# Six warming products, the first top between pair 1's two projections, and batch 1's feature sums as two VectorE instructions

## The chip, the cores and the metric

One core of a Trainium2 chip runs the whole kernel. Its engines are TensorE (PE, with its weight loads listed apart as PEld), VectorE (DVE), ScalarE (ACT), GpSimd (POOL) and SyncE (SP, which issues most DMAs). Each engine runs its own instructions strictly in the order in which the program lists them, and waits for the others through semaphores. The metric is the time of one execution on the device in microseconds, as the median of several runs; less is better.

## The reference

The input x is eight batches of 512 features by 1024 tokens; a 0/1 mask says for each token whether it is kept. Every batch gets one layer of attention with eight heads of 64 features, in which queries, keys and values are the same projection, and the result is added to x:

```python
xt = jnp.transpose(x, (0, 2, 1))
q = xt @ Wq.T
qh = q.reshape(B, T, NH, dk).transpose(0, 2, 1, 3)
scores = scale * jnp.einsum('bhqd,bhkd->bhqk', qh, qh)
logits = (scores * cmask + (1.0 - cmask) * NEG) * rmask
attn = jax.nn.softmax(logits, axis=-1)
ctx = jnp.einsum('bhqk,bhkd->bhqd', attn, qh)
out = ctx.transpose(0, 2, 1, 3).reshape(B, T, D) @ Wo.T
x = x + jnp.transpose(out, (0, 2, 1))
```

A token that is masked out as a query has all logits 0, so it attends to all tokens alike: its context is the projection of the mean token. A masked key gets no weight from the kept queries.

## The kernel before

About half of the tokens are kept, so the kernel gathers the kept tokens of each batch (at most 544) beside one column with the mean token, and does the attention on these alone. The work goes pair by pair: a pair is two heads (128 features) of one batch, so there are 4 pairs in a batch and 32 in all; pair number p below counts them through (pairs 0 to 3 are batch 0).

Ahead of the loop `early` works out the ranks of the kept tokens, turns batch 0 into token rows in DRAM (`turn_first`), and turns Wq on PE (`turn_weights`). `warm(n, block)` is n transposes of a block into a PSUM bank that nobody reads: PE work that computes nothing. There are three calls of seven, six and sixteen, and a last one of twenty behind the weights (L1231). `late` begins the main part: `gather` fetches batch 0's kept rows by five indirect DMAs (tile `xin`, issued by POOL, which then makes the masks `part` and issues the loads of batch 1 and of Wo), `put_mean` multiplies and places the mean column, and `collect` turns each gathered block on PE into `xc`, copied out of PSUM by ACT and DVE in turns.

A pair needs, in this order:

- `project(pair, hf)`, twice: four products with Wq for one half of the columns (L593, tile `pq`), and an ACT copy into the ring `qT` (L603, for the second half also L605).
- `values(pair)`: five PE transposes of `qT` (L621), copied by ACT into `v` (L627, L628).
- `lengths_of(pair)`: an ACT square of `v` (L638), the DVE sums by head (L640, tile `len`) and their maximum (L647, tile `top`).
- `bias_of(pair)`: `turn_top` turns the top on PE (L650), DVE takes the maximum and makes the bias of the exponentials (L659 to L662). This must stand ahead of the pair's first exponential.
- `scores(pair, c)` for five key blocks in the order 4, 0, 1, 2, 3: score products on PE (L701 for the short last block, L679 for the others) and the exponentials on ACT (L704, L687, tile `e`), each of which frees the PSUM buffer of its scores. There are two buffers of two banks.
- the products of exponentials and values (L725 and L743, tile `av`), spread over the next pair's blocks, DVE's inverses of the sums (L819 to L836), whose rows go through DRAM (SP), and the output.

The loop runs over pairs p and, inside, over k = 0 to 4, the place in the block order. At each k it issues first the scores, then the tasks that `slots_of(p)` has listed for this k, then pieces of later batches by tables keyed (pair in batch, k): loads, `turn` (DVE transposes L474, tile `xt`, and their stores to DRAM), `search` (DVE counting, L527), `gather`. So the order on each engine is written out by hand. For the mean token of batch b, the 1024 tokens of each feature are summed: `add_features(b, i)` is one ACT pass over 128 features and 512 tokens with an accumulator (L493, tile `junka`), eight of them for a batch. They run four and four: for batch 1 at (p, k) = (0, 3) and (1, 3), for later batches beside other pairs. Batch 0's sums are made instead by DVE, two instructions over 128 x 4 x 512 elements (L427 in `mean_first`). `mean_of` adds the two halves.

For pair 0, `late` runs both projections, the values, the lengths, both projections of pair 1 and then the bias; `slots_of(0)` gives pair 0's slots `values` of pair 1 at k = 0, its lengths and the first half of pair 2's projection at k = 1, and so on.

Of the kernel before, what the change touches and what calls it, by code (L numbers as in the profile page):

```python
# [10 lines left out]
F32 = mybir.dt.float32  # L11
# [295 lines left out]
def attention_of_kept_tokens(ctx, tc, x, mask, wq, wo, out, ident, wqT, woT, verdict, flag):  # L307


    nc = tc.nc  # L310
# [118 lines left out]
    def warm(n, block):  # L429
        pt = bank("warm")  # L430
        for i in range(n):
            nc.tensor.transpose(pt[:, :P], block, ident)
# [55 lines left out]
    def add_features(b, i):  # L488
        r, d = divmod(i, ND)
        if i == 0:  # L490
            xbars[b] = sb.tile([P, ND, NN], F32, tag="xbar", name=f"xbar_{b}")
        junk = sb.tile([P, NB], F32, tag="junka", name=f"junka_{b}_{i}", bufs=1)
        nc.scalar.activation(junk, xs[b][r][:, d, :], AF.Copy, accum_out=xbars[b][:, d, r : r + 1])  # L493

    def mean_of(b):

# [504 lines left out]
    def slots_of(p):  # L1001

        b, pr = pairs[p]
        todo = [[] for _ in range(NC)]
        before = pairs[p - 1] if 0 < p < len(pairs) - 1 else None
        behind = pairs[p + 1] if p + 1 < len(pairs) else None
        ahead = pairs[p + 2] if p + 2 < len(pairs) else None

        def do(k, f, *args):
            todo[k].append(lambda: f(*args))  # L1010

        late = p == 2
        new = pr == 2 and b + 1 < B
        by_vector = nc.vector.tensor_copy

        def project_with_values():
            project(ahead, 0, lambda end: turn_values(behind, end))
            copy_values(behind)

        def mean_with_values():  # L1020
            pt = bank(f"mean_{b + 1}")
            turn_values(behind, pt[:, KH : KH + P])
            put_mean(b + 1, pt, lambda: copy_values(behind))

        def project_with_top(hf, tag="t"):
            project(ahead, hf, lambda to: turn_top(behind, to), tag)
            bias_of(behind)

        if before:
            do(0, go_on_attend, before)  # L1030
        due = []
        if pr == 1 and b + 1 == B:
            due = [0, 1]
        elif pr > 0 and 0 < b < B - 1:
            due = {1: (0, 1, LAST), 2: (2,), 3: (3,)}[pr]
        if not new:
            for i in due:
                do(3, output, b - 1, i)
        if p == 0:
            do(0, values, behind)  # L1040
            do(1, lengths_of, behind)
            do(1, project, ahead, 0)
            do(2, project, ahead, 1)
            do(3, bias_of, behind)
        elif late:
            do(1, values, behind)
            do(2, lengths_of, behind)
            do(2, end_attend, before)
            do(2, put_mean, b + 1)
            do(2, collect, b + 1, 0)  # L1050
            do(3, bias_of, behind)
            do(3, collect, b + 1, 1, by_vector, "a")
            do(3, collect, b + 1, 2, None, "a")
            do(4, collect, b + 1, 3)
            do(4, collect, b + 1, 4)
            for hf in range(2):
                do(4, project, ahead, hf, None, "a")
        elif new:
            do(1, mean_with_values)
            do(2, end_attend, before)  # L1060
            do(3, collect, b + 1, 0, by_vector)
            do(3, collect, b + 1, 1, by_vector)
            do(3, collect, b + 1, 2, by_vector, "a")
            do(3, collect, b + 1, 3, None, "a")
            do(3, collect, b + 1, 4, by_vector)
            do(3, lengths_of, behind)
            for i in due:
                do(3, output, b - 1, i)
            do(3, project_with_top, 0)
            do(3, project, ahead, 1, None, "a")  # L1070
        elif ahead:
            do(1, project_with_values)
            do(2, lengths_of, behind)
            do(2, end_attend, before)
            do(3, project_with_top, 1)
        elif behind:
            do(1, output, b - 1, LAST - 1)
            do(1, values, behind)
            do(2, lengths_of, behind)
            do(2, end_attend, before)  # L1080
            do(3, bias_of, behind)
            do(3, output, b - 1, LAST)
        if p == ND - 1:
            for d in range(ND):
                do(3 + d // 2, turn_weights, woT, "wo", d, None, "at"[d // 2], True)
        if pr == 1 and b + 1 == B:
            do(4, output, b - 1, 2)
        if p + 1 == len(pairs):
            for i in range(NC):
                do((1, 1, 2, 3, 4)[i], begin_output, b, i)  # L1090
        return todo
# [30 lines left out]
    def early(n):  # L1122
# [105 lines left out]
            order_columns(e, nc.vector.tensor_copy if e % 2 else nc.scalar.copy)  # L1228
        for d in range(ND):
            turn_weights(wqT, "wq", d, nc.vector.tensor_copy if d % 2 else nc.scalar.copy)  # L1230
        warm(20, weights["wq"][ND - 1][:, 0:P])  # L1231

    def place_all():

# [22 lines left out]
    def late(n):  # L1257
# [13 lines left out]
            project(pairs[0], hf)  # L1271
        values(pairs[0])
        lengths_of(pairs[0])
        for hf in range(2):
            project(pairs[1], hf)
        order = [LAST, *range(LAST)]
        bias_of(pairs[0])

# [23 lines left out]
        for p, pair in enumerate(pairs):  # L1302
# [3 lines left out]
            for k, c in enumerate(order):  # L1306
                scores(pair, c)
                if k == 1:
                    add_ends(pair)
                if k == 0 and p > 1:  # L1310
                    contexts(pairs[p - 2])
                if k == 0 and before:
                    if p + 1 < len(pairs):
                        invert(before)
                    else:
                        inv = inverses(before)
                if p + 1 == len(pairs):
                    if k == 1:
                        spread(before, inv)
                        contexts(before)  # L1320
                if b > 1:
                    for i in FETCH.get((pr, k), ()):
                        keep_step(pair, c)
                        fetch(b - 2, i)
                if b + 1 == B:
                    for i in FETCH_LAST.get((pr, k), ()):
                        keep_step(pair, c)
                        fetch(b - 1, i)
                for i in (GATHER if b else GATHER_LATER).get((pr, k), ()) if b + 1 < B else ():
                    keep_step(pair, c)  # L1330
                    gather(b + 1, i)
                if k == 3 and (p == 0 or pr in (1, 3)):
                    to = b + 2 if pr == 3 else b + 1
                    for i in range(G) if to < B else ():
                        add_features(to, (G if pr == 1 else 0) + i)
                for task in todo[k]:
                    task()
                if b + 1 < B:
                    at = TURN if b else TURN_LATER
                    if pr < 2 and (pr, k) in at:  # L1340
                        turn(b + 1, at.index((pr, k)))
                    if pr == 1 and k == 4:
                        mean_of(b + 1)
                    for i in () if b else LATER.get((pr, k), ()):
                        search(b + 1, i)
                    if pr == 2 and k == 2:
                        queries_of(b + 1)
                if b + 2 < B:
                    if pr == 3 and (pr, k) in TURN:
                        turn(b + 2, TURN.index((pr, k)))  # L1350
                    for i in LOAD.get((pr, k), ()):
                        load_piece(b + 2, i)
                    if pr == 1 and k == 4:
                        load_ranks(b + 2)
                    for i in SEARCH.get((pr, k), ()):
                        search(b + 2, i)
                if b > 0:
                    for i in (ROWS if b + 1 < B else ROWS_LAST).get((pr, k), ()):
                        load_rows(b - 1, i)
                if p == 0 and k == 1:  # L1360
                    place_all()
                if p == 1 and k == 4:
                    turn_places()
                if b > 1:
                    for i in FINISH.get((pr, k), ()):
                        finish_blocks(b - 2, i)
                if b + 1 == B:
                    for i in FINISH_LAST.get((pr, k), ()):
                        finish_blocks(b - 1, i)
                issue_stores()  # L1370
                while rests:
                    rests.popleft()()
                    if b + 1 < B:
                        break
# [129 lines left out]
```

## Time and profile before

| | |
|---|---|
| median of 3 runs | 659.57 us (658.69 to 660.84) |
| the profiled execution | 660.24 us; span from first to last instruction 658.5 us |
| busy over the span | PE 618.8 us (94%), PEld 383.9, DVE 355.7, ACT 383.6, POOL 212.0 |
| granted PE clock, mean | 0.98 |
| DMA | 116.61 MB, 177 GB/s over the span |
| last 20 warming products | start 25.6 to 27.7 us |
| four `junka` passes each | from 49.3 us and from 63.9 us |

The profile is one execution. A row of the timeline has the start and length in microseconds, the engine, the line of the kernel, the operation, the tile written and the tiles read, the shape, and the count of instructions merged into it. In brackets stand the idle time of the engine just ahead of the row and what released it, as far as the semaphore events tell; "issue" is a wait for nothing that the profile shows, "remote" one without a releaser among the core's instructions. Matrix products of float32 show as two rows each on PE, and their ends are modelled.

### The profile page before, as it was taken

To read this page: it belongs to the slowest core of one execution; us is meant where nothing else is said; L and a number is where in the kernel's file an instruction comes from. 1 tells how busy PE (TensorE), PEld (TensorE's weight loads), DVE (VectorE), ACT (ScalarE), POOL (GpSimd) and SP (SyncE) were. 2 spreads that over 40 slices of the span, in tenths; PEclk is the share of its full clock that TensorE was granted. 3 is DMA by queue.
4 is the path that set the end of the run, shared out by engine and by line. 5 is a ranking of instruction groups with operands and counts; after the bars stand their busy time and mean duration, and the time that the engine had idled before them with its cause. 6 is when DMAs were issued, how large, how long until landed. Compare 5 with 4: busy or idle time off the path is not lost. (4 is left out here: it accounts for less than half of the span.)

```text
span 658.5 us, 15960 instructions
## 1 busy us (share of the span) xinstructions
PE 618.8 (94%) x6092; PEld 383.9 (58%) x6092; DVE 355.7 (54%) x1032; ACT 383.6 (58%) x1020; POOL 212.0 (32%) x313
## 2 busy tenths in 40 slices
PE   5799799999999999999999999999999999998963
PEld 4765476656665666556665666566665666554422
DVE  5545566434475666746475548565665425435542
ACT  4268558755766567754776577655775466553400
POOL 5620500150067003830166004720275006205331
PEclk9999899999999999999999999999999999999975
DMA  8556622354488657977599666975795636477776
GB/s 244 176 199 162 222 69 66 113 193 132 134 177 218 231 176 191 189 242 228 169 180 274 196 189 151 205 249 180 200 174 156 196 102 102 101 178 179 123 219 195
DMA packets 94542, 116.61 MB, mean 177 GB/s; under 512 B 11911, under 2 KB 61639, under 8 KB 94462
## 3 DMA queue, kind: packets, MB, share of 16 engines
q1 hardware_dynamic: 74030, 75.20, 38.6%
q0 software_dynamic: 16208, 38.25, 25.1%
q10 hardware_dynamic: 4224, 2.10, 1.1%
q8 instruction: 49, 0.80, 0.5%
q14 instruction: 31, 0.25, 0.1%
HBM read 72.81 MB, written 42.70 MB: 175 GB/s over the span
## 5 line engine op out<-in xcount | busy, mean ns | idle before, releaser
L687 ACT ACTIVATE e<-s,bias 128x544 f32<-128x544 f32 x256 | 180.5, 710 | 73.6 <-PE s L679 60.2
L679 PE MATMUL s<-qT 64*64 64x272 f32 x2048 | 155.0, 398 | 5.5 <-ACT e L687 3.8
L743 PE MATMUL av<-e,v 64*64 64x272 f32 x1920 | 132.2, 392 | 0.0
L593 PE MATMUL pq<-xc,wqT 128*128 128x272 f32 x512 | 131.3, 401 | 0.0
L593 PEld LDWEIGHTS pq<-xc,wqT 128*128 128x128 f32 x512 | 93.3, 190 | 36.9 <-issue 20.6
L679 PEld LDWEIGHTS s<-qT 64*64 64x64 f32 x2048 | 77.3, 133 | 54.8 <-ACT e L687 12.4
L878 PE MATMUL po<-woT,cT 128*128 128x512 f32 (+1 forms) x448 | 108.9, 439 | 0.0
L889 POOL DMA_DIRECT2D od<-oc x56 | 30.2, 544 | 236.5 <-ACT oc L887 235.7
L972 POOL DMA_INDIRECT g<-od,block_origin x56 | 90.1, 1610 | 29.4 <-DVE ends L716 8.3
L743 PEld LDWEIGHTS av<-e,v 64*64 64x64 f32 x1920 | 76.5, 134 | 38.1 <-issue 2.1
L659 DVE TENSOR_REDUCE m<-pq 128x1 f32<-128x128 f32 x28 | 8.2, 292 | 136.4 <-ACT qT L605 111.9
L878 PEld LDWEIGHTS po<-woT,cT 128*128 128x128 f32 (+1 forms) x448 | 46.5, 149 | 54.6 <-issue 53.2
L603 ACT COPY qT<-pq 128x272 f32<-128x272 f32 x64 | 24.6, 385 | 69.5 <-PE pq L650 28.2
L942 DVE STREAM_TRANSPOSE xr<-g 128x512 f32<-128x512 f32 x56 | 58.0, 1101 | 7.1 <-DMA g<-od,block_origin 7.1
L640 DVE TENSOR_REDUCE len<-sq 128x10 f32<-128x640 f32 x32 | 25.7, 804 | 59.2 <-ACT sq L638 59.2
L969 POOL COPY step<-e 1x1 f32<-1x1 f32 x75 | 24.0, 320 | 96.5 <-ACT e L687 96.4
L687 ACT ACTIVATION_READ_ACCUMULATOR e<-s,bias 128x1 f32 x256 | 50.5, 197 | 0.0
L539 POOL DMA_INDIRECT xin<-xd,source x40 | 39.1, 978 | 16.0 <-DMA woT<-in_L_cond_Wq_dram 5.8
L887 ACT COPY oc<-po 128x512 f32<-128x512 f32 (+1 forms) x35 | 18.0, 515 | 44.0 <-PE po L878 43.1
L493 ACT ACTIVATE junka<-x 128x512 f32<-128x512 f32 x56 | 35.2, 629 | 1.3
L474 DVE STREAM_TRANSPOSE xt<-x 128x1024 f32<-128x1024 f32 x28 | 34.8, 1241 | 0.7 <-issue 0.2
L527 DVE TENSOR_SCALAR_CACHE_REDUCE junk<-rank,key 128x1024 f32<-128x1024 f32 (+4 forms) x35 | 34.9, 997 | 0.0
(174 smaller groups left out, 674.6 us busy)
## 6 DMA issues: line engine op xcount, KB each, us to landing
xd<-xt SPq DMA_DIRECT2D x120, 128.0 KB
x<-in_x_dram SPq DMA_DIRECT2D x56, 256.0 KB
g<-xd SPq DMA_DIRECT2D x56, 256.0 KB
out_dram<-xr SPq DMA_DIRECT2D x28, 512.0 KB
rb<-row SPq DMA_DIRECT2D x60, 160.0 KB
od<-oc POOLq DMA_DIRECT2D x28, 256.0 KB
rank<-ranks SPq DMA_DIRECT2D x6, 512.0 KB
x<-in_x_dram POOLq DMA_DIRECT2D x8, 256.0 KB
```

The source lines that it names most:

```text
L474: nc.vector.transpose(xt.rearrange("p k (d f) -> p k d f", d=ND), xs[b][r][:, :, at : at + n].rearrange("p d (k t) -> p k d t", t=Q),)
L493: nc.scalar.activation(junk, xs[b][r][:, d, :], AF.Copy, accum_out=xbars[b][:, d, r : r + 1])
L527: nc.vector.tensor_scalar(junk[:, :n], rank[:, i * P :], key[:, col], 0.0, ALU.is_le, ALU.add, accum_out=found[:, col])
L539: nc.gpsimd.indirect_dma_start(out=xin[:n, :], out_offset=None, in_=xds[b], in_offset=bass.IndirectOffsetOnAxis(ap=searches[b][2][:n, i : ...
L593: nc.tensor.matmul(pq[:, :KH], wqT[:, d, pr * P : (pr + 1) * P], xcs[b][:, d, cols], start=(d == 0), stop=(d == ND - 1),)
L679: nc.tensor.matmul(ss[h][r * DK : (r + 1) * DK, hf, :KH], qT[heads[h], c * P + r * DK : c * P + (r + 1) * DK], qT[heads[h], queries[hf]], ...
L687: nc.scalar.activation(e[:, :, h, :], ss[h][:, :, :KH], AF.Exp, bias=bias, scale=SCALE, accum_out=sums[pair[1] % 2][:, h, c : c + 1],)
L743: nc.tensor.matmul(avs[pair][hf][head, :KH], v[keys, c, head], e[keys, hf, h, :], start=(c == 0 and not crossed), stop=(c == LAST - 1 and ...
L878: nc.tensor.matmul(po[k * n : (k + 1) * n, :w], cTs[b, pr][:, i * P : i * P + n], woT[:, pr, k * w : (k + 1) * w], start=(pr == 0), stop=( ...
L889: nc.gpsimd.dma_start(ods[b][places[i], k * w : (k + 1) * w], oc[k * n : (k + 1) * n, :w])
L942: nc.vector.transpose(xr.rearrange("p (d a) (t i) -> p a d t i", a=A, i=NT)[..., i], gs[b, i].rearrange("p (a d f) -> p a d f", a=A, f=Q),)
L972: nc.gpsimd.indirect_dma_start(out=gs[b, i], out_offset=None, in_=ods[b], in_offset=bass.IndirectOffsetOnAxis(ap=block_origin[:, b, i : i ...
```

## The change

Four edits, all ahead of or inside pairs 0 and 1 of batch 0:

- The last warming call has six transposes instead of twenty.
- In `late`, only the first half of pair 1's projection stands ahead of pair 0's bias. The second half becomes a task of pair 0's slot k = 0, behind the scores of the last block, and `values` of pair 1 moves from k = 0 to k = 1, behind the first full block of scores and ahead of pair 1's lengths.
- The eight ACT passes over batch 1 (`add_features`) go. From batch 2 on nothing changes.
- A new `sum_features` makes batch 1's sums by one DVE instruction for each half of the tokens, of the shape of batch 0's: at (p, k) = (0, 3) and (1, 1), each behind the `turn` of that place, if it has one, and ahead of the `search`.

In the order of each engine as built, PE has the top's transpose and the short block's scores ahead of the second half of pair 1's projection, and the first full block of scores ahead of pair 1's values; ACT has the copies in the order that follows from this and eight passes less; DVE has the first sum between pair 1's bias and the transpose that follows it, and the second between the last transpose of batch 1 and its first search. POOL and SP keep their order.

```diff
+    def sum_features(b, r):
+        if r == 0:
+            xbars[b] = sb.tile([P, ND, NN], F32, tag="xbar", name=f"xbar_{b}")
+        nc.vector.tensor_reduce(xbars[b][:, :, r], xs[b][r], axis=AX.X, op=ALU.add)
...
         if p == 0:
-            do(0, values, behind)
+            do(0, project, behind, 1)
+            do(1, values, behind)
             do(1, lengths_of, behind)
             do(1, project, ahead, 0)
             do(2, project, ahead, 1)
...
-        warm(20, weights["wq"][ND - 1][:, 0:P])
+        warm(6, weights["wq"][ND - 1][:, 0:P])
...
         lengths_of(pairs[0])
-        for hf in range(2):
-            project(pairs[1], hf)
+        project(pairs[1], 0)
         order = [LAST, *range(LAST)]
         bias_of(pairs[0])
...
-                if k == 3 and (p == 0 or pr in (1, 3)):
+                if k == 3 and p > 1 and pr in (1, 3):
                     to = b + 2 if pr == 3 else b + 1
                     for i in range(G) if to < B else ():
                         add_features(to, (G if pr == 1 else 0) + i)
...
+                    if (p, k) in ((0, 3), (1, 1)):
+                        sum_features(b + 1, p)
```

## The prediction

> **What bounds the kernel now.** I read the table of windows first, cut where the stages change: it tells where TensorE (PE) is not full.
>
> ```profile
> 44.00:54.00 10.00, 7.83 (x89) 4.28 (x85) 5.20 (x16) 8.02 (x24) 0.00 (x0) 1.00 0.45 111
> 54.00:70.00 16.00, 14.92 (x191) 9.64 (x187) 10.07 (x28) 12.74 (x36) 1.07 (x2) 1.00 0.64 180
> 70.00:75.50 5.50, 2.31 (x29) 1.10 (x21) 4.98 (x23) 1.33 (x3) 4.38 (x8) 1.00 0.74 231
> 75.50:79.00 3.50, 3.44 (x32) 1.79 (x34) 0.50 (x4) 2.77 (x9) 1.97 (x3) 0.51 0.42 148
> 90.00:590.00 500.00, 497.94 (x5179) 309.17 (x5175) 275.11 (x818) 319.33 (x859) 156.56 (x220) 1.00 0.66 175
> ```
>
> The columns are the stretch, its length, then the busy time of PE, PE's weight loads, VectorE (DVE), ScalarE (ACT) and GpSimd (POOL), then the granted PE clock, the DMA share and GB/s. From 90 to 590 us PE is busy 497.94 of 500 us: nothing but PE order sets the pace there, so an instruction stream that reaches 90 us earlier also ends earlier by as much. All edits of the change lie ahead of 70 us, the batch-0 head, where PE has holes: 2.2 us in 44 to 54, 1.1 in 54 to 70, and 3.2 in 70 to 75.5. I then read the timeline of those stretches for what ended each hole.
>
> **Part 1, six warming products instead of twenty.**
>
> ```profile
> 19.89 3.67 PE L432 MATMUL warm<-ident,woT 128*128 128x128 f32 x16 [9.15 <-DMA woT<-in_L_cond_Wq_dram]
> 25.61 2.35 PE L432 MATMUL warm<-ident,wq_in_order 128*128 128x128 f32 x20
> 27.79 0.29 PE L566 MATMUL mean<-mean,within 128*128 128x16 f32 x2
> 27.93 2.31 PE L552 MATMUL xc<-ident,xin 128*128 128x128 f32 x20
> 30.17 3.94 PE L593 MATMUL pq<-xc,wqT 128*128 128x272 f32 x16
> 24.20 0.94 POOL L539 DMA_INDIRECT xin<-xd,source  x1 [0.30 <-issue]
> 25.44 0.87 POOL L539 DMA_INDIRECT xin<-xd,source  x1 [0.30 <-issue]
> 28.39 0.96 POOL L401 TENSOR_SCALAR part<-count,kept 64x272 f32<-64x272 f32 x1 [1.05 <-DMA xin<-xd,source]
> ```
>
> The mean's product and the collects stand right behind the warming products in PE's order, without a hole. Twenty start within 27.79 - 25.61 = 2.18 us, 0.109 us apiece, so fourteen fewer free 1.53 us. That is the most it can bring. What is late next are the gathers: five indirect DMAs, 1.25 us apart, the last handed over at 25.44. POOL's second `part` sits behind them and came free at 28.39, so the last landing lies just ahead of that. Collect 3 begins twelve slots behind 27.93, at 29.24 now and at 27.71 without the fourteen; its gather was issued one step ahead of the last and lands between about 27.1 (one step before) and 28.35. I take 28.0, a gain of 1.25; the bounds are 0.9 (both gathers land together at the end) and 1.5 (no wait).
>
> The clock is the other thing these products touch. The first sixteen take 3.67/16 = 0.23 us each, the twenty 0.118: the array came to full rate before the first of the twenty that are cut, so six or twenty are the same to it in this execution.
> The Trainium skill ("TensorE: Matmul & The Clock Gate", Part 4: PE-mode transpose) says that transposes do not engage the full clock, since they do not count as PE work in the same way. By that rule the products would run at the slow 0.23 us and fourteen would be worth 3.2 us, making the sum some 1.7 us better; the rows disagree, since a run of nothing but transposes ended twice as fast as it began.
>
> **Part 2, the first top ahead of pair 1's second projection.**
>
> ```profile
> 34.96 3.83 PE L593 MATMUL pq<-xc,wqT 128*128 128x272 f32 x16
> 37.57 0.16 DVE L647 TENSOR_REDUCE top<-len 128x1 f32<-128x10 f32 x1
> 38.63 0.27 PE L650 MATMUL top<-ident,top 128*128 128x128 f32 x1
> 39.78 0.71 ACT L704 ACTIVATE el<-s,bias 128x544 f32<-128x544 f32 x1 [0.42 <-DVE bias L662]
> 40.15 1.53 PE L679 MATMUL s<-qT 64*64 64x272 f32 x16
> 43.64 1.15 PE L679 MATMUL s<-qT 64*64 64x272 f32 x16
> ```
>
> Now PE runs both halves of pair 1 (1.9 us each) while ACT and DVE make the top, which is ready at 37.73, 2.77 us after the first half starts. With only one half as cover PE stands still for 2.77 - 1.9 = 0.87 us, plus the 0.05 of a handover. What comes back: the top is turned 0.8 us earlier relative to the head, so the first exponential on ACT too, and the full-block scores no longer wait for it to free their PSUM (1.53 against the usual 1.15: 0.38). The values of pair 1 move behind the first scores, so their two ACT copies and the square stand behind two exponentials instead of ahead; ACT reaches that square at nearly the old time, but what PE needs next (buffers of those scores) is there. Net on PE: +0.9 - 0.38, about +0.55 us, a loss. Bounds: +0.9 (nothing comes back) and -0.4 (if ACT, which gets its first exponential 0.8 earlier, is what sets the pace, half of that reaches PE).
>
> **Part 3, the feature sums leave ACT.**
>
> ```profile
> 49.33 0.62 ACT L493 ACTIVATE junka<-x 128x512 f32<-128x512 f32 x1
> 52.21 0.69 ACT L687 ACTIVATE e<-s,bias 128x544 f32<-128x544 f32 x1
> 50.24 1.30 PE L743 MATMUL av<-e,v 64*64 64x272 f32 x14
> 53.05 0.69 PE L701 MATMUL s<-qT 64*64 64x272 f32 x8 [1.51 <-ACT e L687]
> 63.86 0.62 ACT L493 ACTIVATE junka<-x 128x512 f32<-128x512 f32 x1
> 66.74 0.36 ACT L603 COPY qT<-pq 128x271 f32<-128x271 f32 x1
> 65.78 1.15 PE L743 MATMUL av<-e,v 64*64 64x272 f32 x16
> 68.01 0.69 PE L701 MATMUL s<-qT 64*64 64x272 f32 x8 [1.08 <-ACT e L687]
> ```
>
> Twice four ACT sums (49.33 to 52.21, 63.86 to 66.74, 2.88 us each) stand in ACT's order ahead of the exponentials of the last block, and twice PE waits for exactly those exponentials to free a score buffer: 1.51 and 1.08 us. Without the sums the exponential starts when its scores are there: the `av` products at 50.24 show that PE had issued them by then, so it starts over 1.5 us earlier and frees the buffer while PE is still at those products, which end at 51.54 (at 66.93 in the second place). Both waits go: -1.51 and -1.08. That is the firmest term; it cannot bring more than the waits, since PE has work up to them.
>
> What it adds is two DVE sums.
>
> ```profile
> L427 DVE TENSOR_REDUCE xbar<-x x2: 2277/2278/2280, 16.1 to 18.3; 128x4 f32<-128x2048 f32 x2
> 48.71 0.23 DVE L662 TENSOR_SCALAR bias<-pens,m 128x5 f32<-128x5 f32 x1
> 48.84 1.24 DVE L474 STREAM_TRANSPOSE xt<-x 128x1024 f32<-128x1024 f32 x1
> 53.72 0.17 DVE L822 TENSOR_TENSOR sums<-sums,share 128x8 f32<-128x8 f32 x1 [3.54 <-ACT e L687]
> 55.04 1.25 DVE L474 STREAM_TRANSPOSE xt<-x 128x1024 f32<-128x1024 f32 x1 [0.16 <-issue]
> 57.02 1.24 DVE L474 STREAM_TRANSPOSE xt<-x 128x1024 f32<-128x1024 f32 x1
> 61.88 0.82 DVE L640 TENSOR_REDUCE len<-sq 128x10 f32<-128x640 f32 x1 [2.25 <-ACT sq L638]
> 62.73 0.17 DVE L647 TENSOR_REDUCE top<-len 128x1 f32<-128x10 f32 x1
> 64.30 0.27 PE L650 MATMUL pq<-ident,top 128*128 128x128 f32 x1
> ```
>
> 2.28 us each, the same shape as batch 0's. The first goes ahead of the transpose at 48.84, the second behind the one at 57.02; the cover is DVE's idle time ahead of 53.72 (3.54 us) and of 61.88 (2.25). Behind the first are queued a transpose, pair 0's inverses (their rows go out over SP) and two more transposes; behind the second the first search, pair 2's lengths and its top, which PE turns at 64.30. I followed DVE through from these rows: pair 1's bias ends at 48.94 - 0.7 (parts 1 and 2) = 48.2, the sum at 50.5, a transpose at 51.8, pair 0's inverses 1.3 later (53.72 to 55.04) at 53.1, a transpose at 54.3, the end sums 0.8 later (56.29 to 57.02) at 55.1, a transpose at 56.4, the sum at 58.7, the first search 1.4 later (58.26 to 61.88 - 2.25) at 60.1, lengths and top at 61.1. PE asks for that top at 64.30 - 0.7 - 1.5 = 62.1. Hidden, with 1 us to spare; each microsecond that DVE is later than that costs PE one. The stores, searches and gathers of batch 1 run through DVE, SP and POOL earlier or at most half a microsecond later than now, and its collects stand at 80 us and beyond. Cost taken: 0, bounds 0 and +1.
>
> **The hole that I cannot place.**
>
> ```profile
> 69.89 1.10 PE L679 MATMUL s<-qT 64*64 64x272 f32 x16
> 74.17 0.71 ACT L687 ACTIVATE e<-s,bias 128x544 f32<-128x544 f32 x1 [4.60 <-remote]
> 75.03 2.36 PE L679 MATMUL s<-qT 64*64 64x272 f32 x14 [3.19 <-ACT e L687]
> ```
>
> Pair 2's first scores end at 70.99 and nothing else is needed for their exponential, but ACT starts it at 74.17, released by nothing that the profile names. PE stands 3.19 us, and the clock is then granted at half for 3.5 us (the row 75.50:79.00, 0.51), about 3.5 x 0.49 = 1.7 us of work lost. No edit touches an instruction of this place; the likeliest is that it happens again at the same instructions, wherever they now lie. Cost taken: 0.
>
> **The sum.** -1.25 + 0.55 - 1.51 - 1.08 + 0 = -3.3 us. The profiled execution took 660.24 us (a span of 658.5 and 1.7 around it), so its like would take 656.9; it lies 0.67 above the median of the runs, 659.57, and against that median I forecast 656.3. The bounds of the parts add up to -0.9 + 0.9 - 2.6 + 1 = -1.6 and -1.5 - 0.4 - 2.6 = -4.5, that is 655.1 to 658.0.
>
> **The rivals.**
>
> *The hole swallows it.* If ACT waits at 74.17 for something that does not move with PE (transfers are on their way at that time: DMA 0.74 busy), all that is gained ahead of 70.99 only makes the hole longer: 6.5 us instead of 3.2, and the time stays 659.6. For it: the release is unnamed, and the stretch is the only one before 590 us in which PE stands over 2 us. Against: every transfer there is issued by engines that themselves follow PE and ACT, so it would move along.
>
> *The hole goes.* If it comes of a coincidence, the shift may dissolve it: 3.2 and the 1.7 of half clock on top, 656.3 - 4.9 = 651.4. For it: nothing in the order of instructions demands it. Against: the three runs lie within 2.2 us, so such a hole does not come and go between them.
>
> *DVE becomes late.* If its idle time is not there as I counted (the third transpose must find its buffer stored by SP, and the stores of the second go out later than now), pair 2's top comes 2 to 3 us later than I counted, of which 1 is to spare; PE waits for it at what is 64.30 now, and 1 to 2 us of part 3 are given back: 657.8, between 657.3 and 658.3.
>
> *The clock is lost (slower).* The head gets a new hole of 0.9 us between the projection and the top, another of some 0.3 in the collects, and 1.5 us less of steady products ahead of them. If the array then falls to half rate in the projections, each 3.5 us of it costs 1.7 us, as behind 75.5: two such stretches take the whole gain, and from the third on it is slower, 656.3 + 5.1 = 661.4. Against: 1.51 us of idle ahead of 53.05 left the eight products there at 0.69 us in all, the time that eight take at 68.01; only the 3.19 us were followed by a slow stretch.
> The Trainium skill ("TensorE: Matmul & The Clock Gate", Part 1: The HAM clock gate) has the array start throttled and fall back to half after an idle window of about 3.4 us; by that rule, too, holes of 0.9 us are too short.
>
> *It does not do what it says* has little room: the order of the instructions built from the changed file shows six products, the top between the two projections, and both sums on DVE where I placed them; the orders of POOL and SP stay as they are.
>
> **How the numbers follow.** The forecast has 0.57, the hole swallowing it 0.16, the hole going 0.11, DVE late 0.08, the clock lost 0.08. About 0.3%, 2.0 us, can be told from no change here, so faster means below 657.6. Of the forecast's 0.57 some 0.50 lies below that, with all of the hole going (0.11) and 0.03 of DVE late: 0.64. The same are 0.07 of the forecast, 0.11 of the swallowed (the runs scatter by 1 us around it), 0.05 of DVE late: 0.23. Slower is what is left, 0.13: the clock and an ill scatter around 659.6. The range reaches from below the forecast's best bound (655.1, with 1 us of scatter and 1 us of a shorter hole below it) to above the swallowed case: 653.0 to 660.5. Left out are the hole going (0.11) and the clock lost (0.08).
>
> **What would show it.** Right: the projection's first product at about 28.9 instead of 30.17; a PE wait near 36 us of 0.9, ended by DVE's top, and no longer 1.53 but 1.15 for the first full scores; no PE wait over 0.3 us ahead of pair 1's and pair 2's last-block scores, which begin at about 50.9 and 64.8; both DVE sums at 2.3 us with an idle DVE soon behind each; pair 2's first scores at 66.6 and the hole behind them as long as now. Wrong: the hole ends at about 74 or is gone; PE waits for pair 2's top; products behind the head at twice their time; or PE not full from 90 to 590, which would break the step from the head to the end.

## The result, and the profile after

The changed kernel took 655.68 us (median of 13 runs, 652.10 to 657.50) beside 659.57 for the kernel before on the same chip (13 runs, 655.87 to 660.84): a ratio of 0.9942, 95% interval 0.9924 to 0.9959, so 0.6% faster, or 3.9 us (2.7 to 5.0). The forecast was 656.3. The profiled execution took 656.09 us with a span of 654.4.

The table of windows of the changed kernel, cut where its stages now lie (columns as in the prediction):

```profile
44.00:54.00 10.00, 9.34 (x117) 5.43 (x109) 8.67 (x21) 6.12 (x19) 0.00 (x0) 1.00 0.30 69
54.00:67.00 13.00, 13.00 (x161) 8.76 (x163) 12.23 (x27) 9.56 (x26) 1.16 (x2) 1.00 0.70 186
67.00:73.00 6.00, 1.78 (x23) 0.98 (x17) 4.61 (x22) 1.12 (x3) 3.69 (x8) 1.00 1.03 384
73.00:77.00 4.00, 3.98 (x40) 2.04 (x40) 0.00 (x0) 3.26 (x9) 1.86 (x2) 0.57 0.28 95
90.00:590.00 500.00, 497.42 (x5188) 308.82 (x5184) 275.60 (x816) 320.66 (x862) 156.44 (x220) 1.00 0.65 176
```

The 2.2 us of PE holes in 44 to 54 are now 0.66, from 54 to 67 there is none, and the hole that could not be placed stands at 67 to 73, longer than before and with a slow stretch (0.57) behind it as before. From 90 to 590 PE is as full as it was.

The timeline of the changed kernel, first the head (ahead of it, for comparison, the turning of the weights in the kernel before):

```profile
23.36 2.41 PE L1113 MATMUL wq_t<-ident,wq_in_order 128*128 128x128 f32 x16
```

```profile
20.14 3.68 PE L432 MATMUL warm<-ident,woT 128*128 128x128 f32 x16 [11.98 <-DMA woT<-in_L_cond_Wq_dram]
23.61 2.86 PE L1119 MATMUL wq_t<-ident,wq_in_order 128*128 128x128 f32 x16
26.30 0.82 PE L432 MATMUL warm<-ident,wq_in_order 128*128 128x128 f32 x6
26.96 0.29 PE L571 MATMUL mean<-mean,within 128*128 128x16 f32 x2
27.10 2.31 PE L557 MATMUL xc<-ident,xin 128*128 128x128 f32 x20
29.34 3.93 PE L598 MATMUL pq<-xc,wqT 128*128 128x272 f32 x16
```

Six products fill 0.66 us of start times (26.30 to 26.96), and the mean and the collects follow without a hole. The first projection starts at 29.34 instead of 30.17. The weights' turning began 0.25 us later in this execution and took 2.86 us instead of 2.41, so the last warming call starts 0.69 us later (26.30 against 25.61). The longer turning is the clock's doing. The windows around the moment at which it becomes full in the changed kernel:

```profile
25.00:25.50 0.50, 0.50 (x4) 0.50 (x3) 0.00 (x0) 0.29 (x1) 0.34 (x1) 0.50 0.57 229
25.50:26.00 0.50, 0.50 (x7) 0.50 (x6) 0.44 (x1) 0.00 (x0) 0.50 (x1) 0.97 0.78 172
```

PE goes from four to seven products per half microsecond. In the trace's clock records the full clock begins at 25.53 here and at 24.39 in the kernel before; counted from the first of the sixteen warming products that is 5.39 against 4.50 us.

The moved top:

```profile
34.13 2.00 PE L598 MATMUL pq<-xc,wqT 128*128 128x272 f32 x8
36.73 0.16 DVE L652 TENSOR_REDUCE top<-len 128x1 f32<-128x10 f32 x1
37.04 0.29 PE L655 MATMUL top<-ident,top 128*128 128x128 f32 x1 [0.92 <-DVE top L652]
37.89 2.10 PE L598 MATMUL pq<-xc,wqT 128*128 128x272 f32 x8
39.92 1.15 PE L684 MATMUL s<-qT 64*64 64x272 f32 x16
43.53 1.15 PE L684 MATMUL s<-qT 64*64 64x272 f32 x16
```

PE stands 0.92 us for DVE's top, and the first full scores take 1.15 instead of 1.53. At the second full scores (43.53, before 43.64) only 0.11 of the 0.83 us gained at 29.34 is left: the edit cost 0.72.

The feature sums:

```profile
48.73 2.28 DVE L498 TENSOR_REDUCE xbar<-x 128x4 f32<-128x2048 f32 x1
50.98 0.45 PE L706 MATMUL s<-qT 64*64 64x272 f32 x2
54.45 1.25 DVE L474 STREAM_TRANSPOSE xt<-x 128x1024 f32<-128x1024 f32 x1 [0.94 <-DMA xd<-xt]
57.62 2.25 DVE L498 TENSOR_REDUCE xbar<-x 128x4 f32<-128x2048 f32 x1
62.01 0.16 DVE L652 TENSOR_REDUCE top<-len 128x1 f32<-128x10 f32 x1
62.44 0.27 PE L655 MATMUL pq<-ident,top 128*128 128x128 f32 x1
64.89 0.64 PE L706 MATMUL s<-qT 64*64 64x272 f32 x8
```

Both last-block scores (50.98 and 64.89) stand without a bracket: the waits of 1.51 and 1.08 us are gone. PE is now 3.1 us ahead of the kernel before (64.89 against 68.01). DVE's third transpose waits 0.94 us for its buffer to be stored, so pair 2's top is ready at 62.17 and PE takes it up at 62.44.

The hole:

```profile
66.73 1.10 PE L684 MATMUL s<-qT 64*64 64x272 f32 x16
71.88 0.71 ACT L692 ACTIVATE e<-s,bias 128x544 f32<-128x544 f32 x1 [5.48 <-remote]
72.74 2.32 PE L684 MATMUL s<-qT 64*64 64x272 f32 x14 [4.22 <-ACT e L692]
```

It is at the same instruction and 1.03 us longer (4.22 against 3.19). PE comes out of it 2.29 us ahead (72.74 against 75.03) and is still 2.25 ahead when the loop is over (`worst_t` at 631.77 against 634.02). The rest of the 4.15 us between the two profiled executions comes in the last stores and fetches, which no edit touches: from the scores near 599 to the end of the span it is 58.7 us in the one and 56.9 in the other, and 55.9 to 59.0 in the twelve profiles of the experiments, none of which has the hole. That this is scatter is likely but not shown: the two profiles of the kernel before have the longest stretches (58.7 and 59.0), the other twelve 55.9 to 57.4.

### The profile page after: what moved, and what is told of

Same layout as the page of the kernel before. It is cut to its first block, busy times and chain, and to the rows that moved or that the text cites. A ratio compares the mean times of both kernels' runs of the same rounds, so it can differ in the third digit from the quotient of the medians.

```text
span 654.4 us, 15913 instructions
## 1 busy us (share of the span) xinstructions
PE 614.3 (94%) x6078; PEld 380.5 (58%) x6078; DVE 359.8 (55%) x1034; ACT 378.3 (58%) x1004; POOL 211.1 (32%) x313
## 5 line engine op out<-in xcount | busy, mean ns | idle before, releaser
L692 ACT ACTIVATE e<-s,bias 128x544 f32<-128x544 f32 x256 | 180.5, 710 | 75.6 <-PE s L684 58.9
L721 DVE CUSTOM_DVE_ANT_0 junk<-el,part 128x272 f32<-128x272 f32 x64 | 27.3, 427 | 6.6 <-ACT el L709 4.4
```

What stands on the lines that cost most here:

```text
L692: nc.scalar.activation(e[:, :, h, :], ss[h][:, :, :KH], AF.Exp, bias=bias, scale=SCALE, accum_out=sums[pair[1] % 2][:, h, c : c + 1],)
L721: nc.vector.tensor_tensor_reduce(junk[:, :KH], e[:, 0, h, :], parts[b], 1.0, 0.0, ALU.mult, ALU.add, ends[pr % 2][:, h : h + 1])
```

## The experiments

Each comparison was made on one chip, with its own runs of the kernel before; the chips differ from one comparison to the next. In the position table, read from the profiles' timelines, the first column is the time from the first of the sixteen warming products to the first projection, the second from there to the product for batch 1's mean (near 72 to 80 us), the third from there to the same late score products, at 590 to 600 us.

| kernel | warming to projection | projection to batch 1's mean | mean to the late scores |
|---|---|---|---|
| before, first measurement | 10.28 | 50.07 | 519.60 |
| changed, first measurement | 9.20 | 48.60 | 519.55 |
| before, again | 9.95 | 45.31 | 519.50 |
| six products alone | 9.74 | 45.33 | 519.56 |
| moved top alone | 9.60 | 46.02 | 519.46 |
| VectorE sums alone | 10.48 | 42.26 | 519.97 |
| changed, second and third comparison | 9.40, 9.21 | 42.97, 42.98 | 520.60, 519.64 |
| changed without moved top, three times | 9.30, 9.42, 8.86 | 42.25, 42.25, 42.26 | 519.46, 519.53, 521.03 |
| the same, batch 2's loads later | 9.20 | 42.26 | 519.50 |
| the same, ranks later too | 9.56 | 42.26 | 519.50 |
| changed, batch 2's loads later | 8.85 | 42.98 | 519.49 |

### Each edit alone

*Six warming products, nothing else.*

```diff
-        warm(20, weights["wq"][ND - 1][:, 0:P])
+        warm(6, weights["wq"][ND - 1][:, 0:P])
```

> The kernel before with one edit: six warming products instead of twenty. Theory A (parts add up, the hole behind pair 2's first scores stays at 3.2 us): the first projection starts about 1.0 us earlier (relative to the start of the sixteen warming products), the wait ahead of pair 1's last-block scores stays near 1.5 us, and the time falls by 0.9 us. Theory B (the hole grows by a third of what is gained ahead of it, as it did from 3.19 to 4.22 us between the two profiles for 3.16 us gained): hole 3.5 us, time down by 0.6 us. Theory C (the waits for the ACT exponentials take the gain back, because ACT's order, not PE's, sets the pace up to 53 us): the wait of 1.51 us grows by up to 0.9 and the time stays within 0.3 us of before.

653.00 us against 653.63, ratio 0.9991 (0.9980 to 1.0003). Its timeline:

```profile
28.22 0.99 PE L552 MATMUL xc<-ident,xin 128*128 128x128 f32 x8 [0.75 <-DMA xin<-xd,source]
29.14 1.18 PE L593 MATMUL pq<-xc,wqT 128*128 128x272 f32 x4
52.03 0.69 PE L701 MATMUL s<-qT 64*64 64x272 f32 x8 [1.52 <-ACT e L687]
```

The time fell by 0.6 us (between 1.3 less and 0.2 more), not by the 0.9 expected, and the first column is 9.74, 0.2 to 0.5 us below the two profiles of the kernel before instead of 1.0. The collect of block 3 waits 0.75 us for its gather, which gives the floor: it goes on at 28.2, the time assumed in the prediction was 28.0, and where a later profile shows such a wait, the collect goes on at 27.8 to 28.6. The wait of 1.52 is as long as before, so theory C falls: a later wait for ACT does not take the gain back, because ACT runs the same steps earlier by as much. Over all profiles the first column is 10.08 on the mean with twenty products (four profiles) and 9.27 with six (ten): 0.8 us, not the 1.53 that the fourteen products fill.

What moves the first column besides is the moment of the full clock. In the four profiles with twenty products it begins 3.10, 3.81, 4.50 and 4.90 us behind the first of the sixteen, and the first column is 9.60, 9.95, 10.28 and 10.48: each microsecond costs 0.49. Set beside this line at their own moments (4.70, 4.71, 5.39 and 5.86 us), the four profiles with six products whose collects do not wait (8.85, 8.86, 9.20 and 9.42) lie 1.5 us below it. So the fourteen products are worth all of their 1.53 us where the gathers are in time; in the other six profiles, where a collect waits, it is 0.1 to 1.0.

*The moved top, nothing else.*

```diff
-            do(0, values, behind)
+            do(0, project, behind, 1)
+            do(1, values, behind)
...
-        for hf in range(2):
-            project(pairs[1], hf)
+        project(pairs[1], 0)
```

> The kernel before with one edit: the first top is turned between pair 1's two projections, whose second half moves behind the first scores. Theory A: a PE wait of about 0.9 us for the top near 37 us, the first full-block scores back from 1.53 to 1.15 us, so PE 0.5 to 0.7 us later at the second full-block scores (43.64 before), and the time up by 0.5 to 0.7 us. Theory C (what ACT gains by starting its exponentials earlier is what counts while the feature sums are still on ACT): the 1.51 us wait ahead of pair 1's last-block scores shrinks by about as much as PE is late, and the time stays within 0.3 us or falls by up to 0.4.

654.21 us, ratio 1.0013 (0.9999 to 1.0028). The timeline:

```profile
37.12 0.29 PE L650 MATMUL top<-ident,top 128*128 128x128 f32 x1 [0.92 <-DVE top L647]
53.01 0.69 PE L701 MATMUL s<-qT 64*64 64x272 f32 x8 [1.51 <-ACT e L687]
```

The wait for the top is there and the 1.51 us wait hasn't shrunk: nothing is given back. The second column is 0.71 us longer than that of the kernel before (46.02 against 45.31), and the medians differ by 0.6 us, which alone can't be told from nothing. Theory A.

*The two VectorE sums, nothing else*: `sum_features` and its two calls, and `add_features` only for p above 1, as in the change.

> The kernel before with one edit: the second batch's feature sums as two VectorE instructions instead of eight ScalarE ones. Theory A: both waits (1.51 and 1.08 us) go, DVE's top of pair 2 is not late, the hole stays 3.2 us: 2.6 us less. Theory B (the hole takes a third of it back): hole 4.0 us, 1.7 us less. Rival D (DVE late: without the 0.1 to 0.7 us of the other two edits DVE has no slack left): PE waits 0.3 to 1 us for pair 2's top at about 64 us, and 1.0 to 1.5 us less in all.

651.32 us, ratio 0.9962 (0.9948 to 0.9975). The timeline, around the first of the two waits and at batch 1's second gathered block:

```profile
51.23 1.07 PE L748 MATMUL av<-e,v 64*64 64x272 f32 x12
52.10 0.45 PE L706 MATMUL s<-qT 64*64 64x272 f32 x2
76.04 1.39 PE L557 MATMUL xc<-ident,xin 128*128 128x128 f32 x8 [0.41 <-DMA xin<-xd,source]
```

The second column falls by 3.05 us (45.31 to 42.26), more than the 2.59 of the two waits, and pair 2's top is not late. The first wait is what brought more than its row: from the first projection, pair 1's last-block scores come 1.94 us earlier for a wait of 1.51. The two traces show why. In the kernel before, the scores start 2.81 us behind the start of the `av` row ahead of them (50.24 to 53.05), whose modelled end lies at 1.30, and the wait is counted from there. Without the wait they start 0.87 us behind the start of that row, 0.43 ahead of its modelled end: 1.51 + 0.43 = 1.94. Of the 3.05 us, 0.47 is lost again behind the mean (third column 519.97): the collect of batch 1's second block waits 0.41 us for its gather.

*Both without the moved top*: the changed kernel with pair 1's projections and values where the kernel before has them.

> The changed kernel without the moved top (six warming products and the two VectorE sums alone). Theory A: the sum of both parts, 3.5 us less than before, 0.6 us less than the changed kernel. Theory B: 2.4 us less by PE's positions behind the hole, 0.4 less than the changed kernel, the rest of it being swallowed by the hole. Theory C (the earlier top is worth something once the sums are off ACT): as the changed kernel or slower, with a longer wait for pair 2's top or for exponentials between 40 and 53 us.

650.13 us, ratio 0.9959 (0.9941 to 0.9976), and by positions 3.06 us in the second column. The parts add up, within the scatter of the medians (3.5 us for both, 0.6 and 2.3 for each).

None of these four profiles has the hole, so theory B (it grows by a third of what is gained) had nothing to act on.

### Is the hole part of the kernel?

*The kernel before, unchanged, once more.*

> The kernel before, unchanged, on the chip on which the parts were run. None of the four parts' profiles shows the hole of 3.2 to 4.2 us behind pair 2's first scores nor the slow stretch behind it. Theory E (the hole belongs to the executions of the first measurement, not to the order of instructions): no hole here either, PE goes on within 0.3 us, and the profiled time is about 653.6 us, some 5 us (3.2 plus 1.7 of half clock) below the first profile's. Theory F (the hole needs the exact stream of the kernel before or of the changed one): the hole is there, 3 us or more, and the time is near 658.

655.84 us in its one execution; the seventeen runs of the kernel before beside it have a median of 653.87. The timeline, at the place of the hole:

```profile
69.99 1.10 PE L679 MATMUL s<-qT 64*64 64x272 f32 x16
71.12 0.71 ACT L687 ACTIVATE e<-s,bias 128x544 f32<-128x544 f32 x1 [1.45 <-PE s L679]
71.97 1.60 PE L679 MATMUL s<-qT 64*64 64x272 f32 x14
75.57 0.40 PE L566 MATMUL mean<-mean,within 128*128 128x16 f32 x2
```

ACT starts that exponential 0.03 us behind the modelled end of the scores, released by PE, and PE goes on without a wait; 14 products take 1.60 us, not 2.36. Up to here the execution agrees with the first profile to 0.1 us; behind it, it is 4.7 us ahead (75.57 against 80.24). So the hole and the slow stretch are no property of the instruction stream alone: the same kernel has them in the first measurement and not here, nor are they in any of the eleven other profiles of the experiments, which come from four chips (the parts above from one, this run from another). On those chips the kernel before takes 653.6 to 654.1 us in the median instead of 659.6. Theory E. Which chip the first measurement was made on isn't known, so whether the hole belongs to a chip or to that measurement stays open.

*The changed kernel, unchanged, and the version without the moved top, side by side, twice.*

> The changed kernel, unchanged, on the same chip. By the parts (the top 0.7 us dearer, the sums 2.4 to 2.6 cheaper, the warming 0.3 to 0.6 cheaper): 2.0 to 2.5 us below the kernel before, if the hole is in neither (theory E). If the larger difference of the first measurement (3.9) was the change's own: 3.5 to 4.3 below. Theory F: hole of 3 us or more in the profile.

> The changed kernel without the moved top, once more beside the changed kernel on one chip. If the moved top costs what its positions show (0.72 us from the first projection to the second full scores, nothing given back): 0.7 us below the changed kernel, 2.7 to 3.3 below the kernel before. If the earlier top is paid back where the profile of one execution can't show it: within 0.3 us of the changed kernel.

| | changed | without the moved top |
|---|---|---|
| second comparison | 652.38 us, 0.9980 (0.9960 to 1.0001) | 649.51 us, 0.9931 (0.9913 to 0.9948) |
| third comparison | 652.64 us, 0.9970 (0.9951 to 0.9990) | 649.51 us, 0.9919 (0.9895 to 0.9943) |

The changed kernel is 1.5 us below the kernel before, not the 3.1 that its three parts make (0.80 - 0.72 + 3.05), and the version without the moved top is 3 us better still, for 0.72 us by positions. Both expectations missed: 2.0 to 2.5 us for the changed kernel, 0.7 between the two. The profile of the changed kernel in the second comparison shows where some of it goes:

```profile
71.67 0.40 PE L571 MATMUL mean<-mean,within 128*128 128x16 f32 x2
73.01 0.63 PE L557 MATMUL xc<-ident,xin 128*128 128x128 f32 x4 [0.94 <-DMA xin<-xd,source]
```

The first collect of batch 1 waits for its gather. That is the 1.1 us by which the third column is longer (520.60). For the second and third side-by-side run the expectations were:

> The changed kernel on one chip with the version without the moved top, to settle what the top costs (0.72 by positions, 2.9 between the medians of the last comparison). Theory G: in the profile of the changed kernel the second batch's collects waited 0.94 us for a gather that took over 7 us to land (issued 65.55, used 73.01), a wait that comes and goes with the transfers, so the difference is 0.7 plus 0 to 1. Theory H: the moved top costs about 2 us or more also here, with a place in the profile that shows it.

> The changed kernel without the moved top, on one chip with the others. Theory G: 0.7 to 1.7 us below the changed kernel and 2.7 to 4 below the kernel before. Theory H: 2 us or more below the changed kernel.

The medians differ by 3.1 us here, beyond theory G's 0.7 to 1.7 and as theory H has it, but the profiles of this comparison (650.36 us for the changed kernel, 652.19 for the other) are the other way round, and the longer wait is in the version without the moved top:

```profile
65.71 1.03 POOL L544 DMA_INDIRECT xin<-xd,source  x1 [1.03 <-DMA x<-in_x_dram]
72.12 0.40 PE L571 MATMUL mean<-mean,within 128*128 128x16 f32 x2
73.91 0.63 PE L557 MATMUL xc<-ident,xin 128*128 128x128 f32 x4 [1.40 <-DMA xin<-xd,source]
77.22 0.96 POOL L401 TENSOR_SCALAR part<-count,kept 64x272 f32<-64x272 f32 x1 [4.16 <-DMA xin<-xd,source]
```

The gather was issued at 65.71 and used at 73.91. In the trace's DMA completions fourteen of its sixteen parts land from 70.4 to 71.0, the fifteenth at 72.2 and the last at 73.8. PE now comes to this place at 72 instead of 75.6 (hole-free) or 80.2 (with the hole), so what had always been early enough is now just in time.

The gathers themselves gain little from the earlier start. In the hole-free profiles with the sums still on ACT the first gather is issued at 68.1 to 69.2 and lands 2.9 to 4.1 us later. With the sums on DVE it is issued at 64.5 to 67.0, and its parts land from 4.3 to 4.8 us behind that, the last of them 5.0 to 8.1 us behind.

### Taking the transfers away that delay the gathers

At this time SP's loads of batch 2's inputs are under way, six of 256 KB ahead of the gathers. Moved behind them:

```diff
+        LOAD_FIRST = {(2, 1): (0, 1, 2, 3), (2, 2): (4, 5, 6, 7)}
...
-                    for i in LOAD.get((pr, k), ()):
+                    for i in (LOAD if b else LOAD_FIRST).get((pr, k), ()):
```

on the version without the moved top:

> The changed kernel without the moved top, and with all eight loads of batch 2's inputs moved behind the gathers of batch 1 (from pair 1's last steps to pair 2's second and third). If these loads (2 KB packets on the same 16 DMA engines until about 70 us) are what makes the gathers take 5 to 7 us to land: the first landing comes 2 us or more earlier after its issue, the waits of the second batch's collects (0.2 to 0.9) go, and the time is 0.2 to 0.9 us lower than without the edit and scatters less. If the gathers' own pace on POOL (1.3 us apart) sets their landing: no change within 0.3. Rival: the third batch's transposes and searches then wait for their loads, and PE for those: 0.5 us or more slower.

650.10 us, ratio 0.9933 (0.9909 to 0.9958). The timeline:

```profile
64.78 1.04 POOL L544 DMA_INDIRECT xin<-xd,source  x1 [0.91 <-PE s L706]
71.31 0.40 PE L571 MATMUL mean<-mean,within 128*128 128x16 f32 x2
71.56 0.64 PE L557 MATMUL xc<-ident,xin 128*128 128x128 f32 x4
74.08 0.97 POOL L401 TENSOR_SCALAR part<-count,kept 64x272 f32<-64x272 f32 x1 [1.93 <-DMA xin<-xd,source]
```

All sixteen parts of the first gather now land between 67.7 and 68.2, 2.9 to 3.4 us behind its issue instead of 4.7 to 8.1, and the collect follows the mean without a wait. The two other profiles with these loads moved, further down, show 2.8 to 3.5. So those loads are what delays the gathers. The Trainium skill ("DMA: Bandwidth & Descriptors", Issuing engines are not separate DMA queues) says that DMAs started by SP, ACT or POOL run on the same sixteen engines and interleave; the trace agrees, with 2.9 to 3.4 us against 4.7 to 8.1. The median, though, stays where it was: of the three earlier profiles of this version only one shows a wait over 0.3 us, and most of its runs lie near 649.5 already. The expected 0.2 to 0.9 us did not show.

With the load of batch 2's ranks moved as well (at p = 2, k = 1 for batch 0):

> As the one before, with the load of batch 2's ranks (128 copies of 4 KB) moved behind the gathers as well. If its 512 KB are the traffic that delays the last two gathers: landings another 0.5 us or more earlier and up to 0.3 us lower than the version before it; if not: the same within 0.3; if batch 2's searches become late: slower by 0.5 or more.

649.53 us, ratio 0.9921 (0.9897 to 0.9945): the same.

The loads moved, the moved top kept:

```diff
+        LOAD_FIRST = {(2, 1): (0, 1, 2, 3), (2, 2): (4, 5, 6, 7)}
...
-                    for i in LOAD.get((pr, k), ()):
+                    for i in (LOAD if b else LOAD_FIRST).get((pr, k), ()):
```

> The changed kernel with its moved top kept, and the eight loads of batch 2's inputs moved behind batch 1's gathers, as in the version before it. Two comparisons put the changed kernel 0.5% (about 3 us) above the version without the moved top, though the positions of PE show only 0.72 us for it up to the second batch's mean. Theory G (the other 2 us are executions in which the second batch's collects wait for a gather of which one part lands 1.5 to 3 us behind the rest, as in two of the profiles): with the loads out of the way the ratio to the kernel before falls to 0.9925 to 0.995, 0.7 us above the version without the moved top. Theory H (the moved top itself costs 3 us in most executions): the ratio stays at 0.997 to 0.998.

649.86 us (649.21 to 651.48), ratio 0.9942 (0.9923 to 0.9960), instead of 652.4 and 652.6 with ratios of 0.9980 and 0.9970. The best executions of the changed kernel lie at 648.7 to 650.1 without the edit too, but 19 of its 24 in the last two comparisons lie beyond 651 us; with it, 2 of 6 do, and none beyond 651.5. Of the version without the moved top and with the loads where they were, 5 of 24 do. The ratio lies where theory G has it: the top itself costs its 0.7 us, and the other 2 us come and go with batch 2's loads. That is supported, not shown: the run was made on another chip than the two it is compared with, and the intervals touch or overlap slightly. Nor does a profile show the 2 us: both hole-free profiles of the changed kernel have a wait for batch 1's gathers (0.94 and 0.37 us), but these executions took 651.05 and 650.36 us, less than the medians, and the version without the moved top has such waits as well (none, 0.21 and 1.40 us in its three profiles). What the executions beyond 652 us wait for, and why there are more of them with the moved top, stays open.

The versions without the moved top, with or without moved loads, beat both kernels: 649.5 to 650.1 us, 3.5 to 4.6 below the kernel before on their chips. With the loads moved, what the moved top still costs (649.86 against 650.10 and 649.53, on different chips) can't be told from nothing.

## Why the prediction was right or wrong

**What bounds the kernel.** Right: an instruction stream that reaches 90 us earlier ends earlier by as much. The third column of the table is 519.46 to 519.64 in eleven of the fourteen profiles, whatever was done ahead of it; the other three (519.97, 520.60 and 521.03) are those with the longest waits for batch 1's gathers (0.41, 0.94 and 1.40).

**Part 1, warming, -1.25.** That the products cost their time and that the gathers cap the gain was right, the size was not: 0.83 us in the first profile, 0.8 on the mean. The floor that the gathers set was placed well (28.0; 28.2 in the profile of this edit alone), but in the first profile it did not bind: no collect waits there. What the term left out is that the warming call itself moves. It took the moment of the full clock from one profile and found that six or twenty products are the same to it; in the changed kernel's profile this moment came 0.89 us later behind the first warming product, which costs 0.44 us, and the weights' turning began 0.25 us later: 1.52 - 0.44 - 0.25 = 0.83. Where the full clock comes sooner, more of the fourteen products are spent waiting for the gather. The projection did not start at 28.9 but at 29.34.

**Part 2, the top, +0.55.** Right in its place (0.92 us near 36 to 37, ended by DVE's top) and in what comes back (1.53 to 1.15). The term was 0.71 to 0.72 wherever it can be read, 0.17 above the forecast and within its bounds.

**Part 3, the sums, -2.59 and 0 for DVE.** The waits went, at 50.98 and 64.89 (forecast 50.9 and 64.8). The term was a little undersized: 3.05. "It cannot bring more than the waits" is the step that failed, since 1.51 us of idle in a row was worth 1.94: the wait was counted from a modelled end that lies 0.43 us behind the moment at which the next product can start. DVE is hidden, with less to spare than the 1 us counted: the buffer wait of the rival, 0.94 us at 54.45, did come, and the top was ready 0.27 us before PE took it up.

**The hole, 0.** The step "the likeliest is that it happens again at the same instructions" held in the first measurement, but not with the length taken: there it was 1.03 us longer, for 3.16 us gained ahead of it, so that 2.3 of the forecast 3.3 us are seen behind it. Whether it grew because of the gain isn't shown. But the argument against its going ("the three runs lie within 2.2 us, so such a hole does not come and go between them") took the runs of one measurement for the kernel. In the profiles from four chips it is not there, and the kernel before is 5 to 6 us faster.

**The sum, -3.3.** It came out near the measured 3.9, and part of that is luck. By positions, the change brought 2.3 us through the loop in the first measurement: a warming term 0.4 too large and the longer hole stand against sums that brought more than their waits. The rest of the profiled difference lies in the last stores and fetches, for which the prediction has no term; what makes up the median's 3.9 us beyond the 2.3 no profile shows. On the four chips, without the hole, the parts make 3.1, of which 1.5 is left. There batch 1's gathers become the next thing late: their waits explain up to 1.4 us of single profiles, and the ratio without these loads in front supports that they are the rest as well. The prediction looked at them ("its collects stand at 80 us and beyond"), but 80 us was the hole's doing: without it the collects stand at 75.8, and after the change at 72.

**The rivals.** *DVE late* and *the clock lost* did not happen: no slow stretch behind the warming products, no wait for pair 2's top. *The hole swallows it* came out by a third, in one pair of profiles. *The hole goes* is what the profiles from the four chips show, for both kernels alike.

## What to carry to other kernels

Before a change is credited with what it takes away, ask what is next at that place and from which time on it is ready: here the gathers of batch 0 capped one edit, and those of batch 1, delayed by loads that nobody was waiting for yet, became the next limit as soon as PE came to them some 3.5 us earlier. A long unexplained hole in one profile should be looked for in a profile from another measurement, on another chip, before it is planned around: it hid that second limit. And an edit whose row says "0.9 us of new waiting, 0.4 given back" is a loss unless the profile names the wait that it shortens; the version without it was better as long as nothing else was moved.

## What the runs showed of the hardware

- The same kernel ran 653.6 to 654.1 us in the median on four chips and 659.6 in the first measurement, where ACT started one exponential 3.2 to 4.1 us behind the modelled end of its scores without a named releaser, followed by about 3.4 us at half clock. What causes this was not found; none of the twelve later profiles has it.
- The clock became full 3.1 to 5.9 us behind the first of the sixteen warming products, not at the same moment in two executions of one kernel (4.50 and 3.81 us for the kernel before), and in the profiles without a gather wait each microsecond of it moved the first projection by 0.49.
- Loads of 1.5 MB in flight on SP's queue stretched the landing of a gather issued by POOL from 2.8 to 3.5 us to 4.3 to 8.1, and single parts of the sixteen lagged the others by up to 2.7 us.
- A wait of 1.51 us in a row of the timeline was worth 1.94 us when it went, because the row ahead of it is shown 0.43 us longer than it holds up the next.
